# Four graph layers on one core: one-hot products split over the panels of a pass, two whole arms behind a branch, and tiles turned ahead of the last product

## The chip, the cores and the metric

The kernel runs on one core of a Trainium2 chip. The metric is the device time of one execution in microseconds. The core has five engines that work side by side, each with its own queue of instructions: TensorE (PE, matrix products, with its weight loads as PEld), VectorE (DVE), ScalarE (ACT), GpSimd (POOL) and SyncE (SP, which here issues DMA transfers). An engine works through its queue in order; an instruction that waits holds up all behind it.

## What is computed

There are N = 2708 nodes with 128 features each and a dense adjacency matrix `adj` (2708 x 2708, mostly zeros). Four graph layers follow one another, each as `x = layernorm(x + layer(x, adj))`. Cut to what matters here:

```python
# layer 0: z from adj @ x, the 4 nearest neighbours by distance, added to adj
# layer 1: attention; the quotient needs adj @ exp(...) for every pair of nodes
XW = X @ W;  s_col = XW @ a[:f];  s_row = XW @ a[f:]
den = exp(leaky_relu(s_row[:, None] + s_col[None, :], 0.01))
num = A @ den
att = where(num != 0, den / where(num != 0, num, 1), 0)
x = layernorm(x + A @ (att @ XW))
# layer 2
d = 1 / sqrt(adj.sum(axis=1) + 1e-6)
x = layernorm(x + (d[:, None] * adj * d[None, :] @ x) @ W.T + b)
# layer 3
x = layernorm(x + relu(concat([x, adj @ x]) @ W.T + b))
```

The kernel uses that `exp(leaky_relu(r + c))` is one of two products of a row factor and a column factor, depending on the sign of r + c. Nodes are ranked by c and cut into 44 blocks of 62 ranks (`NB`, `BJ`). For one block only the rows whose sign changes inside it need their own weights; the rest enter through sums that are carried from block to block.

## The kernel before

The matrix is held transposed in HBM and read in panels of 4 x 128 rows by up to 512 columns (`load_panel`, 1 MB) into a ring of strips; six of the 22 row tiles stay resident (`res`). The columns are cut into six chunks (`C`), four panels each. The stages follow one another:

1. The first pass with the degrees, the products z, the distances and the four nearest of each node (to about 297 us), and a second pass over the panels for layer 0, during which nodes are ranked (to 484 us).
2. **The third pass** (484 to 569 us). For each chunk `part_sum` (L1056) multiplies every panel by `lc`, 32 columns wide, and `end_sums` (L1065 to L1068) copies the sums to `tot`, folds them with the matrix `sel` and stores them as rows of `carry`. Beside it the lists of the blocks are made. The order on TensorE, VectorE and ScalarE is the written one (`tc.manual_schedule`). `into_places(out, at, values)` compares places with a ramp on VectorE (L906) to get one-hot matrices `hot_in`, in four parts over three buffers, and multiplies the values by them on TensorE (L911), 44 matmuls in one go (22 products, two records each). `ranked()` uses it once, behind the first chunk, to get the row numbers `row_j` and the sorted c (`csort`). `find_values()` and `find_places()` then fill `val_b`, the running sums in `counts`, the largest count as `flag`, and the places `pos`. Behind the second chunk `on_all(g_row, csort)` turns csort into a row that all partitions hold (L813, L814); behind the third `listed()` uses `into_places` again and writes `slot_i`, `slot_e`, `slot_f`, and `on_all(gb, rr)` makes another such row. `weights` (L1023 to L1030) fills `lw` behind the third to fifth chunk.
3. **The branch** (L1174, L1175). Every engine reads `flag` into a register. If a block has more than `KC` = 126 rows, a dense arm is run; otherwise the block arm. The dense arm stands first in the program, the block arm in `Else`. With the inputs given the block arm is taken.
4. **The block arm** (574 to 811 us): 2 halves of the columns by 22 pairs of blocks, 44 steps. Each gathers up to 126 rows per block (`load`, L1161, on POOL) and two carry rows (L1167, SP), multiplies them by `lw` (`find_num`, L1227), takes the inverse on ScalarE as Ln and then Exp (`invert`, L1116 and L1117), corrects it on VectorE (`mix_1`, `mix_2`, `mix_3`: L1124, L1128, L1131), and adds the product with `xws` (`add_up`, L1139). Each step has a wide piece (1024 columns) and a narrow one (330). The order on all five engines is the written one. Ahead of the loop stands `nc.scalar.preload_act_table_set("natural_log_exp_and_others")` (L1217), a set of function tables from which both the Ln and the Exp of `invert` run; in the trace it is one `ACT_TABLE_LOAD`.
5. **The turn.** The second half of the sums is copied to `mT` (L1283), 22 tiles are turned on TensorE (L1293) and scaled on VectorE into `mixed` (L1294). Then `dinv` is computed from the degrees with `inv_sqrt` (L1298, L1299; a square root on ScalarE, L232, and a reciprocal on VectorE). These lines stand behind the branch, outside the manual order, so the scheduler places them.
6. Three more passes over the panels (`by_panels`, L190) for layers 1, 2 and 3, each with a normalization per chunk (which takes a square root on ScalarE), to the end at 1149 us.

Of the kernel before, what the change touches and what calls it, by code (L numbers as in the profile page):

```python
# [52 lines left out]
def kernel(  # L53
# [537 lines left out]
    mis_pool = psum.enter_context(tc.tile_pool(name="mis1", bufs=4, space=bass.MemoryType.PSUM))  # L591
# [205 lines left out]
    with tc.tile_pool(name="rank", bufs=1) as rank:  # L797
# [9 lines left out]
        def on_all(row, col):  # L807

            for o in range(0, row.shape[-1], CW):
                e = min(row.shape[-1], o + CW)  # L810
                ps = mis_tile()
                for k in range(o, e, P):
                    nc.tensor.transpose(ps[:, k - o : k - o + P], col[:, k // P : k // P + 1].to_broadcast([P, P]), ident)  # L813
                nc.scalar.activation(row[:, o:e], ps[:, : e - o], AF.Exp, scale=0.99)  # L814
# [82 lines left out]

        parts = [(t, min(t + 6, T)) for t in range(0, T, 6)]

        def into_places(out, at, values):  # L900

            width = values.shape[-1] * values.shape[-2]
            for t0, t1 in parts:
                n = t1 - t0
                hot = hot_in[:, t0 // 6 % 3 * 6 * P : (t0 // 6 % 3 + 1) * 6 * P].rearrange("p (t k) -> p t k", k=P)
                nc.vector.tensor_tensor(  # L906
                    hot[:, :n, :], iota[:, None, :].to_broadcast([P, n, P]),
                    at[:, t0:t1, None].to_broadcast([P, n, P]), op=ALU.is_equal,
                )
                for t in range(t0, t1):  # L910
                    nc.tensor.matmul(  # L911
                        out[:, :width], lhsT=hot[: pw[t], t - t0, :],
                        rhs=values[: pw[t], t, :, :].rearrange("p a b -> p (a b)"),
                        start=(t == 0), stop=(t == T - 1),
                    )
# [10 lines left out]
        def ranked():  # L926

            js = mis_tile()
            into_places(js, b_j, val_q[:, :, :2, :])
            nc.vector.tensor_scalar_add(row_j, js[:, :NQ], float(OOB))  # L930
            nc.vector.tensor_copy(csort, js[:, NQ : 2 * NQ])
            xws = lwx.tile([P, NQ, D], F32, tag="xws", name="xws")
            nc.gpsimd.memset(xws, 0.0)
            nc.scalar.activation(g_col, csort, AF.Exp, scale=0.99)
            nc.scalar.activation(g_inv, csort, AF.Exp, scale=-0.99)
            return xws
# [61 lines left out]
        def listed():  # L998


            sl = mis_tile()
            into_places(sl, pos, val_b)
            lw = lwx.tile([P, NB, BJ + 2], F32, tag="lw", name="lw")
            in_turn = sl[:, : 3 * NB].rearrange("p (v chain m) -> p v m chain", v=3, m=CH)
            for h in range(2):
                nc.vector.tensor_scalar(
                    slot_i[h].rearrange("p (m chain) -> p m chain", m=CH), in_turn[:, 0], 2.0, 2.0 * OOB + h,
                    op0=ALU.mult, op1=ALU.add,
                )

            for n, (v, at) in enumerate(((slot_e, KC), (slot_f, KC + 1))):
                nc.vector.tensor_scalar_add(
                    v.rearrange("p (m chain) -> p m chain", m=CH), in_turn[:, n + 1], ident[:, at : at + 1]
                )
                nc.vector.tensor_copy(lw[:, :, n], v)
            return lw
# [55 lines left out]

        for c in range(C):
            w = cw[c]
            for i0 in range(0, FULL, 4):
# [8 lines left out]
                if (c, i0) == (0, 8):  # L1084
                    find_sel()
                    find_blocks()
            if c % GROUPS == 0:
                for n in range(c, c + GROUPS):
                    part_sum(n, FULL, 0, res[few(n), FULL - S, cols[n]], few(n), last=n == c)
            if c == 0:  # L1090
                count()
                xws = ranked()
                find_values()
                find_places()
            if c == 1:
                g_row = wide.tile([P, NQ * P], F32, tag="wide", name="g_row")
                on_all(g_row, csort)
            if c == 2:
                lw = listed()
                gb = big.tile([P, N], F32, tag="hT", name="gb")  # L1100
                on_all(gb, rr)
            if 2 <= c < C - 1:
                weights(lw, g_row, range((c - 2) * 16, min((c - 1) * 16, NB), 2))
# [69 lines left out]
    mT = wide.tile([P, N], F32, tag="wide", name="mT")  # L1173
    over = nc.values_load(flag[0:1, 0:1], min_val=0, max_val=N)  # L1174
    with tc.If(over > KC) as full:  # L1175
# [36 lines left out]
    with full.Else():  # L1212
        with (
# [40 lines left out]
            with tc.manual_schedule(engines={e.engine for e in engines}):  # L1254
# [4 lines left out]
                for i, (h, q) in enumerate(steps):  # L1259
# [14 lines left out]
                    errs = {}  # L1274
                    for piece, (c0, w, _) in pieces.items():
                        errs[piece] = mix_1(w, nums[i, piece], invs[i, piece], own)
                        keep(i, piece, errs[piece])
                    for piece in pieces:
                        mix_2(invs[i, piece], errs[piece])
                    for piece, (c0, w, _) in pieces.items():  # L1280
                        mix_3(w, q, invs[i, piece], h * HALF + c0)
                add(len(steps) - 1)
                nc.scalar.copy(mT[:, HALF:], haccs[1][:, :HALF])  # L1283

    acc_pool = ctx.enter_context(tc.tile_pool(name="acc2", bufs=3, space=bass.MemoryType.PSUM))
    mis_pool = ctx.enter_context(tc.tile_pool(name="mis2", bufs=5, space=bass.MemoryType.PSUM))

    hT = big.tile([P, N], F32, tag="hT", name="hT")
    mixed = big.tile([P, T, D], F32, tag="y", name="mixed")
    for t in range(T):  # L1290
        p = pw[t]
        pt = mis_tile()
        nc.tensor.transpose(pt[:p, :D], mT[:, t * P : t * P + p], ident)  # L1293
        nc.vector.tensor_scalar_mul(mixed[:p, t, :], pt[:p, :D], f_out[:p, t : t + 1])  # L1294
    spread(mixed[:, FULL, :])


    nc.vector.tensor_scalar_add(dinv, deg, DEG_EPS)  # L1298
    inv_sqrt(dinv, dinv)  # L1299
    y3 = wide.tile([P, T, D], F32, tag="wide", name="y3")  # L1300

    def end_layer1(c, ts):
        for t in ts:
            p = pw[t]
            pt = mis_tile()
            nc.tensor.transpose(pt[:p, :D], hT[:, t * P : t * P + p], ident)
            nc.vector.tensor_add(xs[:p, t, :], xs[:p, t, :], pt[:p, :D])
        normalize(ts, xs)
        for t in ts:
            nc.scalar.mul(y3[: pw[t], t, :], xs[: pw[t], t, :], dinv[: pw[t], t : t + 1])  # L1310
            if t == FULL:
                spread(y3[:, t, :])
            nc.gpsimd.tensor_add(xs[: pw[t], t, :], xs[: pw[t], t, :], bl_sb[: pw[t]])

    by_panels(rows_of(mixed), into_hT(end_layer1))


    own3 = big.tile([P, T, D], F32, tag="y", name="own3")

    def end_layer2(c, ts):  # L1320
        for t in ts:
            p = pw[t]
            po = linear(t, wl_sb)
            nc.vector.scalar_tensor_tensor(
                xs[:p, t, :], po[:p, :D], dinv[:p, t : t + 1], xs[:p, t, :], op0=ALU.mult, op1=ALU.add
            )
        normalize(ts, xs)
        if ts[-1] == FULL:
            spread(xs[:, FULL, :])

    by_panels(rows_of(y3), into_hT(end_layer2))

    for t in range(T):
        p = pw[t]
        pt = mis_tile()
        nc.tensor.transpose(pt[:, :p], xs[:p, t, :], ident[:p, :p])
        xT = small.tile([P, P], F32, tag="z", name="xT")
        nc.scalar.copy(xT[:, :p], pt[:, :p])
        po = mis_tile()
        nc.tensor.matmul(po[:p, :D], lhsT=xT[:, :p], rhs=wx_sb, start=True, stop=True)  # L1340
        nc.vector.tensor_add(own3[:p, t, :], po[:p, :D], bc_sb[:p])

    last = wide.tile([P, T, D], F32, tag="wide", name="last")

    def end_layer3(c, ts):
        for t in ts:
            p = pw[t]
            po = linear(t, wh_sb)
            nc.vector.tensor_add(own3[:p, t, :], po[:p, :D], own3[:p, t, :])
            nc.vector.scalar_tensor_tensor(  # L1350
                last[:p, t, :], own3[:p, t, :], 0.0, xs[:p, t, :], op0=ALU.max, op1=ALU.add
            )
        normalize(ts, last)
        t0, t1 = ts[0], min(ts[-1] + 1, FULL)
        nc.sync.dma_start(out[t0 * P : t1 * P, :].rearrange("(t p) d -> p t d", p=P), last[:, t0:t1, :])
        if t1 <= ts[-1]:
            nc.sync.dma_start(out[FULL * P :, :], last[:LAST, FULL, :])

    by_panels(rows_of(xs), into_hT(end_layer3))


# [32 lines left out]
```

## Time and profile before

| | us |
|---|---|
| median of 14 runs (1141.54 to 1151.47) | 1147.2 |
| the profiled execution | 1150.52 |
| its span, first to last instruction | 1148.8 |
| third pass | 484 to 568.7 |
| block arm, first to last product | 574.3 to 810.1 |
| three last passes | 817.5 to 1141 |
| busy: TensorE / VectorE / ScalarE / GpSimd | 1020.4 / 652.7 / 346.0 / 278.0 |

The profile gives, for each engine, when each instruction ran, for how long, and which instruction or transfer ended the idle time ahead of it. Busy shares over the whole span are averages over stages with different limits, so the windows by stage are of more use. TensorE's clock is granted by a throttle: 1.0 is full speed, and in some stretches of the third pass it was 0.5. `ACT_TABLE_LOAD` is an instruction of ScalarE that brings in a set of function tables (`LoadActFuncSet` in the program).

### The profile page before, as it was taken

How to read it: one execution, taken by the hardware profiler on the slowest of the kernel's cores; microseconds unless marked ns; L12 is line 12 of the kernel's file. 1: busy time of each engine (PE TensorE's matmuls, PEld its weight loads, DVE VectorE, ACT ScalarE, POOL GpSimd, SP SyncE). 2: the span in 40 equal slices, each digit the busy share in tenths (PEclk: the TensorE clock that was granted, in tenths of full speed). 3: DMA queues.
4: the chain of work that ended last, by engine and by line, in shares of the span. 5: the costliest groups of instructions: out<-in, count | busy, mean ns of one | idle time of the engine just before them, and what ended most of it. 6: DMA issues, size and time to landing. Idle time of an engine off the chain costs nothing.

```text
span 1148.8 us, 11369 instructions
## 1 busy us (share of the span) xinstructions
PE 1020.4 (89%) x3651; PEld 489.9 (43%) x3651; DVE 652.7 (57%) x1388; ACT 346.0 (30%) x632; POOL 278.0 (24%) x268
## 2 busy tenths in 40 slices
PE   1899999999945987597589999999899999999997
PEld 0455544444412545344133333333444644465445
DVE  6885459999412555965069989999321221223122
ACT  0000245555001333513266767666010100011000
POOL 4000000001473762000358875663010100000000
PEclk9899999999976988769789999999999999998999
DMA  9986420000644644467635444543657667573854
GB/s 349 364 296 207 141 71 1 1 0 28 219 135 136 208 133 137 146 208 251 199 97 166 145 136 136 160 127 115 218 184 237 191 228 248 154 226 111 270 168 127
DMA packets 109986, 191.67 MB, mean 167 GB/s; under 512 B 13928, under 2 KB 46978, under 8 KB 109918
## 3 DMA queue, kind: packets, MB, share of 16 engines
q1 hardware_dynamic: 91582, 151.86, 40.3%
q0 software_dynamic: 18336, 39.01, 11.6%
q8 instruction: 30, 0.49, 0.2%
q14 instruction: 38, 0.31, 0.1%
HBM read 215.76 MB, written 4.16 MB: 191 GB/s over the span
## 4 chain that ended last, share of the span: by engine, by line
PE 65%; DVE 10%; DMA 8%; another core or an unknown queue 7%; issue 4%; POOL 3%; ACT 3%; SPq 0%; POOLq 0%; DVEq 0%; ACTq 0%
PE acc L190 30%; PE acc L579 8%; PE acc L397 6%; PE num L1227 6%; PE hacc L1139 5%; POOL rows L1161 2%; DVE both L452 2%; PE acc L569 2%; DMA part<-in_adjT 2%; DMA res<-in_adjT 2%; DMA rows<-carry 2%; PE mis L911 1%; DMA xws<-xw_rows,row_j 1%; PE acc L1056 1%
## 5 line engine op out<-in xcount | busy, mean ns | idle before, releaser
L190 PE MATMUL acc<-part,y 128*128 128x512 f32 (+2 forms) x384 | 159.6, 561 | 2.3 <-DMA part<-in_adjT 1.8
L1161 POOL DMA_INDIRECT rows<-in_adjT,slot_i x88 | 126.8, 1441 | 121.2 <-PE num L1227 57.1
L1227 PE MATMUL num<-rows,lw 128*64 128x512 f32 (+1 forms) x528 | 121.0, 564 | 13.3 <-DMA xws<-xw_rows,row_j 7.2
L1139 PE MATMUL hacc<-inv,xws 128*128 128x512 f32 (+1 forms) x264 | 112.1, 560 | 2.4 <-DVE inv L1131 2.0
L579 PE MATMUL acc<-zT,z 128*128 128x512 f32 (+4 forms) x264 | 106.9, 551 | 0.0
L1124 DVE TENSOR_TENSOR err<-inv,num 128x1024 f32<-128x1024 f32 x88 | 74.8, 856 | 50.3 <-ACT inv L1117 47.4
L608 POOL DMA_INDIRECT got<-y_rows,where x88 | 90.1, 1024 | 52.5 <-issue 23.2
L1116 ACT ACTIVATE inv<-num,plain 128x1024 f32<-128x1024 f32 x88 | 80.5, 915 | 70.3 <-PE num L1227 54.1
L190 PEld LDWEIGHTS acc<-part,y 128*128 128x128 f32 x384 | 72.9, 198 | 67.4 <-issue 56.2
L580 ACT COPY key<-acc 128x512 f32<-128x512 f32 (+3 forms) x132 | 70.2, 534 | 58.1 <-issue 29.8
L397 PE MATMUL acc<-part,y 128*128 128x512 f32 (+2 forms) x192 | 82.4, 582 | 3.7 <-DVE y L237 2.2
L1139 PEld LDWEIGHTS hacc<-inv,xws 128*128 128x128 f32 x264 | 46.8, 190 | 80.6 <-issue 50.0
L190 PE MATMUL acc<-part,xs 128*128 128x512 f32 (+2 forms) x192 | 78.8, 553 | 0.2 <-DMA part<-in_adjT 0.2
L1131 DVE SCALAR_TENSOR_TENSOR inv<-gb,g_inv,inv 128x1024 f32<-128x1024 f32 x88 | 77.1, 917 | 0.0
L224 ACT COPY hT<-acc 128x512 f32<-128x512 f32 (+2 forms) x18 | 9.6, 534 | 220.2 <-PE acc L190 220.2
L190 PE MATMUL acc<-part,mixed 128*128 128x512 f32 (+2 forms) x192 | 75.3, 546 | 0.1
L1227 PEld LDWEIGHTS num<-rows,lw 128*64 128x64 f32 x528 | 39.9, 138 | 75.6 <-issue 52.2
L1128 DVE SCALAR_TENSOR_TENSOR inv<-err,inv 128x1024 f32<-128x1024 f32 x88 | 71.8, 856 | 0.0
L579 PEld LDWEIGHTS acc<-zT,z 128*128 128x128 f32 (+1 forms) x264 | 47.0, 186 | 53.8 <-issue 48.4
L541 POOL TENSOR_TENSOR y<-xs,d2inv 128x2176 f32<-128x2176 f32 (+1 forms) x2 | 4.6, 2322 | 265.1 <-ACT d2inv L539 265.1
L1117 ACT ACTIVATE inv<-inv 128x1024 f32<-128x1024 f32 x88 | 67.6, 768 | 2.8
L581 DVE MAX8 near<-key 128x8 f32<-128x2708 f32 (+1 forms) x22 | 65.4, 2971 | 3.4 <-ACT key L580 3.4
(271 smaller groups left out, 1226.7 us busy)
## 6 DMA issues: line engine op xcount, KB each, us to landing
part<-in_adjT SPq DMA_DIRECT2D x102, 1024.0 KB
part<-in_adjT SPq DMA_DIRECT2D x24, 768.0 KB
part<-in_adjT SPq DMA_DIRECT2D x24, 552.0 KB
res<-in_adjT SPq DMA_DIRECT2D x4, 1280.0 KB
got<-y_rows,where POOLq DMA_INDIRECT x88
rows<-in_adjT,slot_i POOLq DMA_INDIRECT x88
rows<-carry SPq DMA_DIRECT2D x88, 10.6 KB
xw_rows<-xwe POOLq DMA_DIRECT2D x1, 1344.0 KB
```

The costliest lines, as they stand in the source:

```text
L190: nc.tensor.matmul(accs[c][: lhsT.shape[-1], :w], lhsT=lhsT, rhs=src, start=start, stop=stop)
L397: nc.tensor.matmul(accs[c][:, : cw[c]], lhsT=y[:, i, :], rhs=src[:, : cw[c]], start=first, stop=last)
L579: nc.tensor.matmul(pks[c][:p, : cw[c]], lhsT=z2[:, :p], rhs=zT[:, cs], start=False, stop=True)
L580: nc.scalar.copy(key[:p, cs], pks[c][:p, : cw[c]])
L608: nc.gpsimd.indirect_dma_start(out=got[:p, :], out_offset=None, in_=y2_rows[:, :], in_offset=bass.IndirectOffsetOnAxis(ap=where[:p, t, k : ...
L1116: nc.scalar.activation(inv, num[:, :w], AF.Ln, scale=plain[:, 0:1], bias=plain[:, 1:2])
L1124: nc.vector.tensor_mul(err, inv, num[:, :w])
L1128: nc.vector.scalar_tensor_tensor(inv, err, 2.0, inv, op0=ALU.subtract, op1=ALU.mult)
L1131: nc.vector.scalar_tensor_tensor(inv, gb[:, col : col + w], g_inv[:, q : q + 1], inv, op0=ALU.max, op1=ALU.mult)
L1139: nc.tensor.matmul(haccs[:, o:e], lhsT=xws[:, q, :], rhs=inv[:, o:e], start=(q == 0), stop=(q == NQ - 1))
L1161: nc.gpsimd.indirect_dma_start(out=rows[i][:KC, n, :], out_offset=None, in_=adj_half[:, :], in_offset=bass.IndirectOffsetOnAxis(ap=slot_i[ ...
L1227: nc.tensor.matmul(num[n * (BJ + 2) : (n + 1) * (BJ + 2), o:e], lhsT=lw[:, 2 * q + n, :], rhs=rows[i][:, n, c0 + o : c0 + e], start=True, ...
```

## The change

Three edits.

- In the third pass `into_places` is split into `ones_at` (the comparisons) and `into_places(..., n)` (the products of one of four parts). A new function `between(c, i0)` is called behind each group of four row tiles and holds all side work: one part behind each panel, `on_all` in pieces of eight or fewer tiles, `find_values` moved ahead of `count`. The results `js` and `sl` get a PSUM pool of their own with one buffer; `mis1` has three buffers instead of four, the second pass included.
- The branch is turned round (`over <= KC`), so the block arm stands first, and all that follows the branch is written out in both arms: `two_layers` holds the turn, dinv, and the layers 1 to 3. Tiles that were allocated anew behind the branch become views of older ones (`hT = gb`, `mixed` of `carry`, `y3` and `last` of `m_rows`, which also holds `mT`).
- In the block arm the first ten tiles (`EARLY`) are turned and scaled, on ScalarE, ahead of the last product; the last step works piece by piece and does not keep carry rows; the copy of the second half is split in three between ScalarE and VectorE.

```diff
-    mis_pool = psum.enter_context(tc.tile_pool(name="mis1", bufs=4, space=bass.MemoryType.PSUM))
+    mis_pool = psum.enter_context(tc.tile_pool(name="mis1", bufs=3, space=bass.MemoryType.PSUM))
+    js_pool = psum.enter_context(tc.tile_pool(name="places", bufs=1, space=bass.MemoryType.PSUM))
...
+        def ones_at(at, n):
+            t0, t1 = parts[n]
+            w = t1 - t0
+            hot = hot_in[:, n % 3 * 6 * P : (n % 3 * 6 + w) * P].rearrange("p (t k) -> p t k", k=P)
+            nc.vector.tensor_tensor(
+                hot, iota[:, None, :].to_broadcast([P, w, P]), at[:, t0:t1, None].to_broadcast([P, w, P]),
+                op=ALU.is_equal,
+            )
+            return hot
+
+        def into_places(out, hot, values, n):
             width = values.shape[-1] * values.shape[-2]
...
+            t0, t1 = parts[n]
+            for t in range(t0, t1):
+                nc.tensor.matmul(
+                    out[:, :width], lhsT=hot[: pw[t], t - t0, :],
+                    rhs=values[: pw[t], t, :, :].rearrange("p a b -> p (a b)"), start=(t == 0), stop=(t == T - 1),
                 )
...
+        def between(c, i0):
+
+            if (c, i0) == (0, 8):
+                find_sel()
+                find_blocks()
+                work["hot"] = [ones_at(b_j, n) for n in range(3)]
+                find_values()
+            if (c, i0) == (0, 20):
+                count()
+                work["js"] = js_pool.tile([P, CW], F32, tag="places", name="js")
+                into_places(work["js"], work["hot"][0], val_q[:, :, :2, :], 0)
+                work["hot"].append(ones_at(b_j, 3))
+                find_places()
+            if c == 1 and i0 < 12:
+                n = i0 // 4 + 1
+                into_places(work["js"], work["hot"][n], val_q[:, :, :2, :], n)
+            if (c, i0) == (1, 8):
+                work["hot"] = [ones_at(pos, n) for n in range(3)]
+                work["xws"] = ranked(work["js"])
+                work["sl"] = js_pool.tile([P, CW], F32, tag="places", name="sl")
+            if (c, i0) == (1, 20):
+                into_places(work["sl"], work["hot"][0], val_b, 0)
+                work["hot"].append(ones_at(pos, 3))
+                work["g_row"] = wide.tile([P, NQ * P], F32, tag="wide", name="g_row")
+                on_all(work["g_row"], csort, 0, 4)
+            if c == 2 and i0 < 16:
+                if i0 < 12:
+                    into_places(work["sl"], work["hot"][i0 // 4 + 1], val_b, i0 // 4 + 1)
+                n0 = (4, 12, 20, NQ)[i0 // 4]
+                on_all(work["g_row"], csort, n0, n0 + 8)
+            if (c, i0) == (2, 8):
+                work["lw"] = listed(work["sl"])
+            if (c, i0) == (3, 4):
+                work["gb"] = big.tile([P, N], F32, tag="hT", name="gb")
+                on_all(work["gb"], rr, 0, 12)
+            if (c, i0) == (3, 8):
+                on_all(work["gb"], rr, 12, T)
+            if (c, i0) in ((2, 20), (3, 20), (4, 20)):
+                weights(work["lw"], work["g_row"], range((c - 2) * 16, min((c - 1) * 16, NB), 2))
...
+                for t0 in range(0, EARLY, WIDE // P):
+                    ts = range(t0, min(t0 + WIDE // P, EARLY))
+                    pt = ops.tile([P, WIDE], F32, tag=f"num{WIDE}", name="pt", bufs=2)
+                    for t in ts:
+                        nc.tensor.transpose(pt[:, (t - t0) * P : (t - t0 + 1) * P], mT[:, t * P : (t + 1) * P], ident)
+                    for t in ts:
+                        nc.scalar.mul(mixed[:, t, :], pt[:, (t - t0) * P : (t - t0 + 1) * P], f_out[:, t : t + 1])
                 add(len(steps) - 1)
-                nc.scalar.copy(mT[:, HALF:], haccs[1][:, :HALF])
...
+                for o in range(0, HALF, CW):
+                    e = min(HALF, o + CW)
+                    evacuate(o // CW + 1, mT[:, HALF + o : HALF + e], haccs[1][:, o:e])
+
+    def two_layers(arm, first):
...
+        hT = gb
+        for t in range(first, T):
             p = pw[t]
             pt = mis_tile()
...
+        nc.vector.tensor_scalar_add(dinv, deg, DEG_EPS)
+        inv_sqrt(dinv, dinv)
+        y3 = m_rows
...
-    with tc.If(over > KC) as full:
...
+    with tc.If(over <= KC) as fits:
+        with ExitStack() as arm:
+            block_layer()
+            two_layers(arm, EARLY)
+    with fits.Else():
+        with ExitStack() as arm:
+            dense_layer()
+            two_layers(arm, 0)
```

## The prediction

> **What bounds the kernel now.** I read in this order: the windows by stage, the chain of waits, ScalarE's groups and waits in the stage of the blocks, and ScalarE's order of time where tables are loaded. Stages first, since the change touches three: the third pass (484 to 568.7 us), the block arm (574 to 810) and the turn into the next product (810 to 817.5). The columns are the stretch, its length, then busy time of TensorE, weight loads, VectorE, ScalarE and GpSimd, the granted clock, DMA share and GB/s.
>
> ```profile
> span 1148.8 us, 11369 instructions
> 600.00:700.00 100.00, 98.65 (x346) 37.35 (x345) 93.36 (x117) 70.60 (x97) 76.89 (x55) 1.00 0.49 144
> 700.00:808.00 108.00, 105.65 (x374) 40.03 (x373) 103.32 (x129) 70.48 (x84) 54.15 (x37) 1.00 0.46 141
> 484.00:568.70 84.70, 68.02 (x414) 30.70 (x414) 39.14 (x106) 21.56 (x54) 11.97 (x10) 0.80 0.69 223
> ```
>
> In the block arm TensorE and VectorE are both full and one step takes 4.9 us (44 steps). ScalarE is busy 70 of 100 us, so it can take about 1.4 us more per step before it is the bound. Its instructions there, by shape (count | busy, mean ns | idle before), and what it waits for (total us, times, longest):
>
> ```profile
> L1116 ACT ACTIVATE inv<-num,plain 128x1024 f32<-128x1024 f32 x40 | 48.2, 1205 | 32.6 <-PE num L1227 27.3 <-DVE err L1124 4.5 <-issue 0.6
> L1117 ACT ACTIVATE inv<-inv 128x1024 f32<-128x1024 f32 x40 | 42.3, 1057 | 1.3
> L1116 ACT ACTIVATE inv<-num,plain 128x330 f32<-128x330 f32 x40 | 25.1, 627 | 28.4 <-PE num L1227 17.5 <-DVE inv L1131 10.3 <-issue 0.6
> L1117 ACT ACTIVATE inv<-inv 128x330 f32<-128x330 f32 x40 | 19.1, 479 | 1.3
> L1271 ACT ACTIVATE xws<-xws,g_col 128x128 f32<-128x128 f32 x19 | 7.3, 386 | 0.0
> ACT inv L1116 <- PE num L1227: 44.8, 57, 2.2
> ```
>
> Now ScalarE in order of time (start, length): where dinv's square root runs, what a table load costs in the stream, and the arm's entry and end.
>
> ```profile
> 157.36 0.23 ACT L232 ACTIVATE dinv<-dinv 128x22 f32<-128x22 f32 x1
> 159.63 1.28 ACT L557 ACT_TABLE_LOAD   x1
> ...
> 479.05 0.24 ACT L691 COPY xwe<-mis 20x129 f32<-20x129 f32 x1
> 479.31 1.28 ACT L804 ACT_TABLE_LOAD   x1
> 480.60 0.22 ACT L804 ACTIVATE e_r<-rr 128x22 f32<-128x22 f32 x1
> ...
> 568.33 0.38 ACT L1068 COPY carry<-mis 88x276 f32<-88x276 f32 x1 [1.91 <-PE mis L1067]
> 574.36 1.28 ACT L1217 ACT_TABLE_LOAD   x1 [5.65 <-issue]
> 578.20 1.20 ACT L1116 ACTIVATE inv<-num,plain 128x1024 f32<-128x1024 f32 x1 [2.56 <-PE num L1227]
> ...
> 803.69 0.48 ACT L1117 ACTIVATE inv<-inv 128x330 f32<-128x330 f32 x1
> ```
>
> The reader should see two things. The 22-column square root, written behind the branch, runs at 157 us, while the square-root table is still active. And inside the arm one load (L1217) serves all 176 logarithms and exponentials: no other load stands between 578 and 804 us.
>
> **The decisive part: where the square root goes.** The changed kernel writes the next layers inside each arm, so dinv cannot be computed ahead of the branch any more. ScalarE's order in the block arm of the changed kernel as built (no profile; L1248 is the preload, L1143 and L1144 are the Ln and Exp of `invert`, which are L1116 and L1117 before):
>
> ```
> L1248 LoadActFuncSet
> L232 LoadActFuncSet
> L232 Activation dinv<-dinv 128x22
> L1143 LoadActFuncSet
> L1143 Activation inv<-num,plain 128x1024
> L1144 LoadActFuncSet
> L1144 Activation inv<-inv 128x1024
> ```
>
> The square root lands between the preload and the loop and evicts the shared table; after it every Ln and every Exp of the loop has a load of its own, 176 in all. The same listing for the kernel before has 7 loads, and the 6 outside the untaken arm are exactly those in its trace, so the listing counts.
>
> Cost of a load: 479.31 to 480.60 is 1.29, and it starts 0.02 after the previous end; 1.31 us each. ScalarE's work from the first of these loads to the last Exp: 176 x 1.31 = 230.6; activations 44 x (1.205 + 1.057 + 0.627 + 0.479) = 148.2; the xws scalings 22 x 0.386 = 8.5, each overlapping its predecessor by about 0.1 (-2.2); one copy of mT 1.3. Sum 386.4, or 8.6 to 8.9 us per step. Before, the same stretch ran from 578.20 to 804.17, 226.0. **+160.4 us.**
>
> Nothing else should be late in that loop. After the narrow Exp, VectorE still has the short product (0.5), the pair of mix_2 (1.55) and the pair of mix_3 (1.75): 3.8 us, while ScalarE spends 4.9 on the next wide pair with its loads. TensorE needs 2.43 + 2.47 per step at full clock. The gathers (POOL) and carry rows (SP) keep their order and get 8.6 us instead of 4.9 per step.
>
> Two rules of the Trainium skill bear on this. "ScalarE: Activation LUTs", What ACT_TABLE_LOAD costs, gives about 2.66 us for each switch, drain included; by it the loads would be 468 us and the kernel near 1531. The row above shows no drain between load and neighbours. "ScalarE activation tables: per-element evaluation and per-set limits", Table sets in the compiler and the runtime, says the back end places loads per block by the greedy longest run; by that one load would serve the loop and the kernel would gain. The listing shows otherwise.
>
> **Third pass.** Of TensorE's order of time, what this part and the turn below rest on:
>
> ```profile
> 497.97 9.74 PE L911 MATMUL mis<-val_q,hot_in 128*128 128x44 f32 x44
> 522.09 0.92 PE L813 MATMUL mis<-ident,csort 128*128 128x128 f32 x6 [3.47 <-ACT g_row L814]
> 531.14 5.41 PE L911 MATMUL mis<-val_b,hot_in 128*128 128x132 f32 x44
> 543.02 1.27 PE L1067 MATMUL mis<-tot,sel 128*88 128x512 f32 x2 [2.90 <-ACT tot L1065]
> ```
>
> The one-hot products (44 in 9.74 us at a granted clock of 0.5, 44 in 5.41 at 1.0) are only moved between panels. VectorE: in_b ends at 496.7; three comparisons 2.7, find_values 4.5, the fourth 0.7 and the running sums and pos 9 bring pos to 513.7 instead of 521.3; with three comparisons and row_j, csort, 516.8. TensorE has its js parts and the second chunk done by about 508.6 and then waits for csort, because sl takes the bank of js: a new wait of 8 us. From there the third chunk, sl and the csort turns take some 13 us; ScalarE's copy tot again stands behind eight weights (2.75, as at 539.75), so the next fold starts near 532.3 instead of 543.0. The rest took 25.7 us and now also holds gb's turns, 2.6: end at 560.6 instead of 568.7, **-8**. Bounds: -16, all of TensorE's waits in this stage, and +2, if the new wait grows and gb's turns run at half clock. The xws clearing on POOL (2.44) moves from 508 to 517, still 30 us ahead of its gathers. The flag, for which SP waited 2.5 us, comes earlier.
>
> **Entry.** From the last carry copy to the first Ln were 9.5 us, 5.65 of them without any wait that the profile shows, in a jump past the dense arm; now the block arm follows the branch directly. But ScalarE first runs two loads and the root, 2.8 us. No row has a branch not taken: between 0 and -6, I take -5, since most of the 5.65 goes and the first product (3.8) becomes the limit. **-5.**
>
> **Turn.** Before, from the last Exp (804.2) to a running product (817.5) were 13.3 us. Now ten of 22 tiles are scaled on ScalarE while VectorE ends: ten x 0.30 = 3.0, three copies one behind the other 1.7, five turns at 0.25 and evictions, 8.3. **-5** (-2 to -8).
>
> **The jump moves to the end** of the arm: SP and VectorE must jump past the dense arm before the kernel ends. 0 to +7.8 (SP's gap at entry, 554.8 to 562.7, is the nearest row); DMA is idle then, I take **+3**. **One PSUM tile fewer** for the second pass: 0 to +4, the waits of TensorE on xwe copies there are 1.3; **+1**.
>
> Sum: 160.4 - 8 - 5 - 5 + 3 + 1 = +146.4. The profiled execution took 1150.5 us, 3.3 above the median 1147.2; it would become 1297, and the median **1293.6**.
>
> **Rivals.**
> - *TensorE becomes the bound at half clock.* It idles 3.7 us of each 8.6 us step; after 1.7 us idle ahead of 496 the clock was 0.5 until 508. At 0.5 its step is 9.8 us: 44 x 9.8 = 431, 45 above ScalarE's sum, 1339. Against it: a TensorE that is always busy got 1.0 in every long stretch.
> - *A drain or refill at each load that the rows of single loads don't show.* Doubling the load, 176 x 1.31 more: 1524. Against it: all six loads measured 1283 ns.
> - *Not slower: the loads cost almost nothing when they come often,* for instance because both tables stay at hand. The place is ScalarE's 1.45 us of waiting per step (60.8 us in 42 steps); below 0.36 us per load all of it hides, and what is left is -8 - 5 - 5 + 3 + 1: 1133. Against it: the same 1283 ns for every load, whichever table it fetched.
>
> **How the numbers follow.** Loads at the row's price 0.90, TensorE at half clock 0.04, doubled loads 0.03, hidden loads 0.03. The time is that of the first. Its range: lowest bounds together 160.4 - 16 - 6 - 8 = +130, 1277; highest 160.4 + 2 - 2 + 7.8 + 4 = +172, 1319, of which the far end needs every bound at once; I give 1277 to 1316. The other three hold 1 in 10 and lie outside. A measurement of this kernel tells apart about 0.2%, 2.3 us: faster 0.03 (hidden loads), same 0.00, slower 0.97.
>
> **What would show it.** Right: some 183 table loads of 1283 ns; ScalarE busy near 570 us instead of 346 and over 95% in the arm; steps of 8.6 to 8.9 us; VectorE and TensorE waiting for L1144. The third pass ending near 561, a fold waiting for tot, and TensorE waiting for csort ahead of sl. Wrong: steps near 4.9 us (loads hidden), near 9.8 with a clock of 0.5 (TensorE), or 13 and more (drain).

## The result and the profile after

The changed kernel took 1300.4 us in the median (1293.6 to 1302.3, 10 runs); the kernel before took 1147.5 beside it (47 runs). The ratio is 1.132, 95% interval 1.129 to 1.135. The change is slower by 153 us, and the profiled span grew by 152.5, from 1148.8 to 1301.3 us.

From the page and from the groups of the changed kernel (count | busy us, mean ns | idle before):

```profile
span 1301.3 us, 11554 instructions
PE 1053.5 (81%) x3651; PEld 497.5 (38%) x3651; DVE 654.0 (50%) x1379; ACT 576.3 (44%) x820; POOL 265.3 (20%) x268
...
L1143 ACT ACT_TABLE_LOAD x88 | 112.9, 1283 | 2.6 <-issue 1.0
L1144 ACT ACT_TABLE_LOAD x88 | 112.9, 1283 | 1.6
```

ScalarE has 188 more instructions, and 177 of them are table loads: one per logarithm, one per exponential, and the square root's own. 2 x 112.9 = 225.8 us of loads are nearly all of its additional 230 us of busy time. ScalarE in order of time, from the last copy of the third pass into one step of the loop:

```profile
569.30 0.38 ACT L1068 COPY carry<-mis 88x276 f32<-88x276 f32 x1 [1.31 <-PE mis L1067]
569.92 1.28 ACT L1248 ACT_TABLE_LOAD   x1 [0.23 <-issue]
571.21 1.28 ACT L232 ACT_TABLE_LOAD   x1
572.50 0.22 ACT L232 ACTIVATE dinv<-dinv 128x22 f32<-128x22 f32 x1
573.76 1.28 ACT L1143 ACT_TABLE_LOAD   x1 [1.04 <-issue]
...
702.95 0.39 ACT L1302 ACTIVATE xws<-xws,g_col 128x128 f32<-128x128 f32 x1
703.35 1.28 ACT L1143 ACT_TABLE_LOAD   x1
704.65 0.63 ACT L1143 ACTIVATE inv<-num,plain 128x330 f32<-128x330 f32 x1
705.29 1.28 ACT L1144 ACT_TABLE_LOAD   x1
706.58 0.48 ACT L1144 ACTIVATE inv<-inv 128x330 f32<-128x330 f32 x1
707.08 1.28 ACT L1143 ACT_TABLE_LOAD   x1
708.38 1.21 ACT L1143 ACTIVATE inv<-num,plain 128x1024 f32<-128x1024 f32 x1
709.60 1.28 ACT L1144 ACT_TABLE_LOAD   x1
710.90 1.06 ACT L1144 ACTIVATE inv<-inv 128x1024 f32<-128x1024 f32 x1
711.86 0.38 ACT L1302 ACTIVATE xws<-xws,g_col 128x128 f32<-128x128 f32 x1
```

The set that holds both functions is loaded at 569.92 and pushed out 1.3 us later by the square root's. From the first load of the loop on, at 573.76, ScalarE has no gap: a step is 8.9 us (702.95 to 711.86), and the end of one instruction and the start of the next are at most 0.02 us apart, loads included. What the others wait for (total us, times, longest), and the stretch of the loop (busy TensorE, weight loads, VectorE, ScalarE, GpSimd, granted clock, DMA share, GB/s):

```profile
DVE err L1151 <- ACT inv L1144: 168.7, 86, 5.6
PE num L1258 <- DVE err L1151: 80.4, 38, 6.6
...
574.00:960.00 386.00, 255.19 (x778) 90.66 (x776) 215.41 (x261) 380.80 (x375) 132.00 (x101) 0.88 0.30 88
```

ScalarE is busy 98.7% of the loop; VectorE waits for it, and TensorE for VectorE. Stage by stage, from the two traces:

| stretch | before | after | difference |
|---|---|---|---|
| start to the first product of the third pass | 486.1 | 490.1 | +4.0 |
| third pass, to the last copy into carry | 82.6 | 79.6 | -3.0 |
| entry, to the first Ln or its load | 9.5 | 4.1 | -5.4 |
| loop, to the last Exp | 226.0 | 386.7 | +160.7 |
| last Exp to the last VectorE instruction | 341.5 | 335.6 | -6.0 |
| to the end of the span | 3.1 | 5.3 | +2.2 |

### The profile page after: what moved, and what is told of

Same layout as the page of the kernel before. It is cut to its first block, busy times and chain, and to the rows that moved or that the text cites. A ratio compares the mean times of both kernels' runs of the same rounds, so it can differ in the third digit from the quotient of the medians.

```text
span 1301.3 us, 11554 instructions
## 1 busy us (share of the span) xinstructions
PE 1053.5 (81%) x3651; PEld 497.5 (38%) x3651; DVE 654.0 (50%) x1379; ACT 576.3 (44%) x820; POOL 265.3 (20%) x268
## 4 chain that ended last, share of the span: by engine, by line
PE 51%; ACT 20%; DVE 10%; issue 9%; another core or an unknown queue 7%; DMA 3%; SPq 0%; POOL 0%; DVEq 0%; ACTq 0%; POOLq 0%
PE acc L190 27%; PE acc L579 7%; ACT L1143 7%; PE acc L397 5%; ACT inv L1144 5%; ACT inv L1143 5%; DVE both L452 3%; PE acc L569 2%; PE acc L1056 2%; DMA part<-in_adjT 2%; DMA res<-in_adjT 1%; DVE where L582 1%; PE mis L263 1%; DVE inv L1155 1%
## 5 line engine op out<-in xcount | busy, mean ns | idle before, releaser
L1258 PE MATMUL num<-rows,lw 128*64 128x512 f32 (+1 forms) x528 | 131.4, 640 | 81.1 <-DVE err L1151 80.4
L1188 POOL DMA_INDIRECT rows<-in_adjT,slot_i x88 | 119.1, 1353 | 261.3 <-PE num L1258 214.2
L1166 PE MATMUL hacc<-inv,xws 128*128 128x512 f32 (+1 forms) x264 | 131.1, 640 | 50.2 <-ACT xws L1302 42.9
L1143 ACT ACT_TABLE_LOAD x88 | 112.9, 1283 | 2.6 <-issue 1.0
L1144 ACT ACT_TABLE_LOAD x88 | 112.9, 1283 | 1.6
L1166 PEld LDWEIGHTS hacc<-inv,xws 128*128 128x128 f32 x264 | 53.2, 216 | 144.7 <-ACT xws L1302 63.5
L224 ACT COPY gb<-acc 128x512 f32<-128x512 f32 (+2 forms) x18 | 9.6, 534 | 219.4 <-PE acc L190 219.4
L397 PE MATMUL acc<-part,y 128*128 128x512 f32 (+2 forms) x192 | 83.6, 590 | 5.4 <-DMA part<-in_adjT 3.2
L190 PE MATMUL acc<-part,y 128*128 128x512 f32 (+2 forms) x192 | 84.6, 577 | 1.9 <-DMA part<-in_adjT 1.4
L190 PE MATMUL acc<-part,carry 128*128 128x512 f32 (+2 forms) x192 | 74.8, 543 | 0.4 <-DMA part<-in_adjT 0.4
L190 PE MATMUL acc<-part,m_rows 128*128 128x512 f32 (+2 forms) x192 | 74.6, 542 | 0.3 <-DMA part<-in_adjT 0.3
```

Of the source, the lines that this page charges most:

```text
L190: nc.tensor.matmul(accs[c][: lhsT.shape[-1], :w], lhsT=lhsT, rhs=src, start=start, stop=stop)
L397: nc.tensor.matmul(accs[c][:, : cw[c]], lhsT=y[:, i, :], rhs=src[:, : cw[c]], start=first, stop=last)
L1143: nc.scalar.activation(inv, num[:, :w], AF.Ln, scale=plain[:, 0:1], bias=plain[:, 1:2])
L1144: nc.scalar.activation(inv, inv, AF.Exp, scale=-1.0)
L1166: nc.tensor.matmul(haccs[:, o:e], lhsT=xws[:, q, :], rhs=inv[:, o:e], start=(q == 0), stop=(q == NQ - 1))
L1188: nc.gpsimd.indirect_dma_start(out=rows[i][:KC, n, :], out_offset=None, in_=adj_half[:, :], in_offset=bass.IndirectOffsetOnAxis(ap=slot_i[ ...
```

## The experiments

Each kernel ran beside the kernel before, on the same chip. That took 1102 to 1106 us beside the first ten kernels and 1143 beside the last two (root_ahead_again, no_early_tiles), where the prediction had 1147; so ratios and differences are compared, and absolute times that were expected on the basis of 1147 are to be read as differences. Below, *the first runs* are those of the result. *Theory A* is that the square root between preload and loop makes 176 loads, and that they are the whole loss. Its rivals: B, the turned branch and the long arms slow the loop; C, TensorE's clock; D, the entry waits for gathered rows whatever else is saved; E, the early tiles replace other waits or don't count; F, a drain at each load.

All traces in one table, in us: the third pass from first product to last copy into carry; entry from there to the first Ln; loop from first Ln to last Exp; last, from the last Exp to the last VectorE instruction.

| kernel | ratio (95%) | third pass | entry | loop | last | end |
|---|---|---|---|---|---|---|
| before_here | | 78.1 | 9.1 | 227.3 | 340.8 | 3.1 |
| after_here | 1.135 (1.129-1.140) | 72.4 | 6.1 | 385.5 | 335.6 | 5.5 |
| root_alone | 1.154 (1.145-1.162) | 78.5 | 10.7 | 385.4 | 339.7 | 3.1 |
| half_the_loads | 1.041 (1.032-1.049) | 69.5 | 4.3 | 274.1 | 334.0 | 5.9 |
| set_loaded_again | 0.989 (0.985-0.993) | 72.9 | 5.0 | 230.4 | 337.0 | 5.6 |
| all_root_ahead | 0.989 (0.986-0.993) | 73.3 | 3.7 | 228.1 | 335.4 | 5.8 |
| root_behind_loop | 0.992 (0.988-0.996) | 68.0 | 3.6 | 226.2 | 335.6 | 5.3 |
| arms_only | 0.997 (0.994-1.000) | 78.5 | 4.5 | 228.2 | 335.6 | 5.9 |
| arms_and_turn | 0.998 (0.996-1.001) | 79.4 | 3.5 | 222.0 | 337.2 | 5.6 |
| third_pass_alone | 0.993 (0.989-0.997) | 72.6 | 11.1 | 225.3 | 340.9 | 3.1 |
| root_ahead_again | 0.993 (0.991-0.996) | 75.4 | 4.0 | 224.4 | 337.2 | 6.3 |
| no_early_tiles | 0.991 (0.987-0.995) | 79.6 | 4.0 | 226.2 | 338.4 | 5.6 |

### The two kernels again

> The kernel before, unchanged, for its stages on this chip. Its profile was taken where the second pass waited some 30 us for copies of hT (TensorE idle from 330 to 352 us), which no experiment's trace shows. Expected: span 1101 us, the third pass from 446 us on and 78.5 us long, entry 10 us, loop 226 to 228 us, turn 11 to 14 us, end 3.1 us.

> The changed kernel, unchanged, for its time and its stages on this chip. Theory A by the stages measured on this chip: 1103 + 159 for the loop (385.4 against 226) - 8.5 for the third pass - 6 for the entry - 5.5 for the turn + 2.3 for the end = 1244 us (ratio 1.128, between 1.122 and 1.136); the third pass at 68 to 73 us with TensorE's last products, and not a late panel, ahead of the last copy to tot. If instead the 10.25 us that the last copy to tot waited belongs to the change, the third pass takes 79 us here too and the time is 1253 us.

Measured: 1108.0 us in one run of the kernel before (1105.7 in the median of the 14 beside it), and 1256.5 for the changed one. The spans differ by 148.3: 1.5 ahead of the third pass, -5.7, -3.0 to the first Ln, +158.2, -5.2, +2.4 and 0.1 of rounding. The third pass gained 5.7 here and 3.0 in the first runs, where the last copy to tot started late; it does not here.

### The square root alone

```diff
         with (dense arm, block arm)
             ...                          # behind the loop, in each arm
+            nc.vector.tensor_scalar_add(dinv, deg, DEG_EPS)
+            inv_sqrt(dinv, dinv)
     (behind the branch)
-    nc.vector.tensor_scalar_add(dinv, deg, DEG_EPS)
-    inv_sqrt(dinv, dinv)
```

> The kernel before with one thing done: the two lines of dinv moved behind the loop inside both arms, outside the written order; nothing else of the change. As built, the root stands at the arm's entry and each Ln and Exp has a table load. Theory A: +160.7 for the loads and 2.8 at entry for two loads and the root, 1147.4 + 163 = 1310, range 1303 to 1317. Rival B (the turned branch or the long arms cost it): 1147 to 1150.

Measured: ratio 1.154, +169 us (interval 160 to 179), 88 + 88 loads, loop 385.4. The branch is not turned and no other part of the change is there, and the loop is the changed kernel's to 0.1 us. B has nothing left to explain. The profiled execution was the fastest of five, and its span is 159 us above that of before_here.

### Half the loads

The order Ln, Exp, Ln, Exp becomes Ln, Ln, Exp, Exp; the square root stays.

```diff
-                    find_inv(i, "narrow")
-                    if i + 1 < len(steps):
-                        find_inv(i + 1, "wide")
+                    both = [(i, "narrow")] + ([(i + 1, "wide")] if i + 1 < len(steps) else [])
+                    for k in both:
+                        invs[k] = own.tile(...)
+                        nc.scalar.activation(invs[k], nums[k]..., AF.Ln, scale=plain[:, 0:1], bias=plain[:, 1:2])
+                    for k in both:
+                        nc.scalar.activation(invs[k], invs[k], AF.Exp, scale=-1.0)
```

> The changed kernel with ScalarE's order in the loop changed from Ln, Exp, Ln, Exp to Ln, Ln, Exp, Exp, so that a step has two table loads instead of four, 90 in the arm instead of 178. Theory A with the loads at 1.31 us each and ScalarE the only bound: a step takes 3.37 + 2.62 + 0.3 (first half) us, 271 us instead of 386.7: 1300.4 - 116 = 1185, range 1178 to 1195. Rival C (TensorE at half clock is the bound): it stays above 1280. Rival F (a drain beside each load that overlaps when they are dense): more than 1200.

Measured: ratio 1.041, 90 loads in the loop (86 fewer). ScalarE's groups there:

```profile
L1301 ACT ACT_TABLE_LOAD x44 | 56.5, 1283 | 0.8
L1305 ACT ACT_TABLE_LOAD x44 | 56.5, 1283 | 0.8
L1301 ACT ACTIVATE inv<-num,plain 128x1024 f32<-128x1024 f32 x43 | 51.8, 1204 | 7.0 <-PE num L1258 7.0
```

The loop went from 385.5 to 274.1, so a load is worth 111.4 / 86 = 1.30 us while ScalarE is the bound, 1.283 of it the instruction. Working the prediction's sum with 90 loads gives 117.9 + 148.2 + 7.6 = 273.7; with its first load the loop took 275.4. Neither F (a drain) nor hidden loads fit. C is out too: by it the time stays that of the changed kernel, above 1280 where the kernel before took 1147, and it fell to 1147.4 beside 1102.0. With 90 loads ScalarE is still the bound, but already waits 7.0 us for TensorE's num.

### The square root elsewhere, or its place kept and the set loaded once more

all_root_ahead moves dinv's two lines ahead of the branch. root_behind_loop puts them at the end of the block arm's written order (and of the dense arm). set_loaded_again leaves them alone and moves one other line:

```diff
-            nc.scalar.preload_act_table_set("natural_log_exp_and_others")
             nums, invs, haccs = {}, {}, {}
 ...
                 find_inv(0, "wide")
+                nc.scalar.preload_act_table_set("natural_log_exp_and_others")
                 for i, (h, q) in enumerate(steps):
```

> The changed kernel with one thing undone: dinv is computed ahead of the branch, so its square root runs early and the arm keeps the shared tables. Theory A (the 176 table loads are the whole loss): the block arm falls back to steps of 4.9 us, 226 us from the first Ln to the last Exp instead of 386.7; 1300.4 - 160.7 - 1.5 (two loads and the root at entry) = 1138, range 1134 to 1143, and 6 table loads in the trace. Rival B (the turned branch or the longer arms slow the block arm itself): steps stay well above 4.9 us, 1200 or more. Rival C (TensorE at half clock is the bound of the arm): it too falls, but the clock in the arm before must then have been near 0.5.

> The changed kernel with the root left inside the arms but written behind the loop, at the end of the arm's written order. Theory A (it is the place of the root, not that it stands in the arm): 1 table load at the arm's entry and one behind the loop, which the normalization then needs no more; within 2 us of the kernel with the root ahead, 1138, range 1134 to 1143. If standing inside an arm is what costs: near 1300.

> The changed kernel with one line moved: the table set that holds both functions is loaded behind the first piece of the first step, and not ahead of the loop; the square root stays where the changed kernel has it, between the third pass and the loop. Theory A (the square root's own set pushes the shared set out, and each Ln and each Exp then gets its own load, because the set last loaded does not hold it): only the first piece loads twice, 174 of 176 loads go, the loop takes 226 + 2.6 = 229 us where it took 386.7, and the time is that of the two kernels with the root elsewhere, 1091 to 1097 us (ratio 0.989 to 0.995). Rival B (the length of the arm or the turned branch is what makes the loop slow): the loop stays near 385 us and the time near 1255 us (ratio 1.138). A second rival, that any square root in the arm spoils the choice of sets for all of the loop: the same, near 1255 us.

Measured: 0.989, 0.992 and 0.989 of the kernel before; the loops take 228.1, 226.2 and 230.4 us. ScalarE of set_loaded_again in order of time:

```profile
521.90 1.28 ACT L232 ACT_TABLE_LOAD   x1 [0.23 <-issue]
523.19 0.22 ACT L232 ACTIVATE dinv<-dinv 128x22 f32<-128x22 f32 x1
525.36 1.28 ACT L1143 ACT_TABLE_LOAD   x1 [1.95 <-issue]
526.66 1.20 ACT L1143 ACTIVATE inv<-num,plain 128x1024 f32<-128x1024 f32 x1
527.88 1.28 ACT L1144 ACT_TABLE_LOAD   x1
529.18 1.06 ACT L1144 ACTIVATE inv<-inv 128x1024 f32<-128x1024 f32 x1
530.25 1.28 ACT L1289 ACT_TABLE_LOAD   x1
531.54 0.63 ACT L1143 ACTIVATE inv<-num,plain 128x330 f32<-128x330 f32 x1
532.20 0.48 ACT L1144 ACTIVATE inv<-inv 128x330 f32<-128x330 f32 x1
532.59 1.19 ACT L1143 ACTIVATE inv<-num,plain 128x1024 f32<-128x1024 f32 x1
```

The root runs where the changed kernel has it, the first Ln and Exp load as they do there, and then one load at 530.25 ends it: 1094.8 us instead of 1256.5 beside it on one chip, 161.7 us for one line. The rival that any square root in the arm spoils the loop is out as well, since in root_behind_loop the arm holds it too. Loads in the loop come from what the last set loaded ahead of it holds, and from nothing else that was changed. These three show what the rest of the change is worth: each beats both kernels.

### The arms and the early tiles

arms_only is the kernel before with the branch turned, both arms to the end and the root ahead of the branch; arms_and_turn adds the ten early tiles and the split copy. no_early_tiles is all_root_ahead without the ten tiles:

```diff
-                for t0 in range(0, EARLY, WIDE // P):
-                    ...                      # ten transposes on TensorE, ten scalings on ScalarE
-            two_layers(arm, EARLY)
+            two_layers(arm, 0)
```

> The kernel before with the branch turned round and both arms written to the end, the root ahead of the branch, no change of the third pass and no tiles turned early. Theory A: the entry gains 5 and the jump at the end costs 2.2, so 1147.4 - 3 = 1144, range 1140 to 1148. Rival D (the entry waits for the gathered rows, not for the jump): the entry gains 0 to 1, and with the jump at the end 1149.

> The same with the ten tiles turned ahead of the last product and the copy split, the third pass still as before. Theory A: 5 less than with the arms only, 1139, range 1135 to 1143; from the last Exp to the running product 8 us instead of 13. The kernel with all three edits should then be another 3 to 8 us below. Rival E (the tiles turned early only take the place of other waits): no more than 1 us below the arms only.

> The kernel of all_root_ahead without the ten tiles turned ahead of the last product (all 22 are turned behind it, in the arm). Theory E (the early tiles give the gain at the turn, 5 us): from the last Exp to the end of the last pass 340.5 us where the kernel with early tiles takes 335.5, and 0.994 of the kernel before. Rival E' (the gain at the turn comes from writing the turn in the arm, where the passes' first products stand behind 6 turned tiles instead of 18; this is what the stages of arms_only, 335.6 us without early tiles, and of arms_and_turn, 337.2 us with them, speak for): 335.5 us, and the same ratio as the kernel with early tiles, within 0.002.

> The kernel of all_root_ahead a second time, to stand beside the next one on the same chip. Theory A: 0.989 of the kernel before, between 0.985 and 0.993.

Measured: arms_only is 3.0 us faster (interval -6.2 to +0.1), arms_and_turn 1.8 (-4.7 to +1.2). In the traces the arms shorten the entry by 4.6 us and the last stretch by 5.2, and lengthen the end by 2.8. The kernels before_here and arms_only ran on different chips, but the other two traces with the old branch, root_alone and third_pass_alone, one from each chip, have 10.7 and 11.1 at the entry and 339.7 and 340.9 in the last stretch, so the chip does not make it. These stages add up to -7.0, more than arms_only gained in time; what takes up the rest is not shown. D falls: the entry does not wait for gathered rows. Without early tiles the last stretch is 335.6 and 338.4 us, with them 334.0 to 337.2, and no_early_tiles is no slower than its neighbour (0.991 against 0.993). So the early tiles are worth nothing that these runs can tell; in the traces the gain comes with the arm. TensorE at the turn, before_here and then arms_only:

```profile
769.64 4.20 PE L1293 MATMUL mis<-ident,mT 128*128 128x128 f32 x18 [1.38 <-ACT mT L1283]
773.68 1.02 PE L190 MATMUL acc<-part,mixed 128*128 128x512 f32 x2
```

```profile
763.98 1.10 PE L1300 MATMUL mis<-ident,m_rows 128*128 128x128 f32 x6 [1.38 <-ACT m_rows L1289]
764.92 1.02 PE L190 MATMUL acc<-part,carry 128*128 128x512 f32 x2
765.78 0.49 PE L1300 MATMUL mis<-ident,m_rows 128*128 128x128 f32 x3
```

Before, 18 of the 22 tiles are turned ahead of the first product of layer 1; in the arm it is six, though all 22 are still turned behind the loop. That accounts for 3.1 of the 5.2 us; the scheduler placed them so, and what in the arm made it was not tried.

### The third pass alone

The changed kernel's lines down to the end of the third pass, with the branch, loop and turn of the kernel before.

> The kernel before with the third pass of the changed kernel (the products in parts between the panels, mis1 with three buffers), and the branch, the loop and the turn as they were. Theory T (the third pass is ended by TensorE's own work and its waits, so whatever is taken out of it is gained): the stretch from the first product of the third pass to the last copy into carry was 78.5, 79.4 and 78.5 us in the three kernels with the old order and 73.3, 68.0 and 69.5 us in the three with the new one on this chip; expected 70 us here, the entry unchanged at 9.5 to 10.7 us, and 1094 us against 1103 of the kernel before (ratio 0.992, between 0.987 and 0.996). Rival D (the block arm's first rows come late whatever the third pass does): the entry grows by what the pass loses, and the time stays at 1103 (0.998 to 1.002). Theory A expects 0 table loads in the loop and the loop at 222 to 228 us, since the square root stays behind the branch.

Measured: ratio 0.993, 8.0 us faster (3.2 to 12.7); the pass 72.6 us against 78.1, the entry 11.1 against 9.1. D, by which the entry takes the whole gain back, is excluded. Beside a kernel before of 1102 to 1106 us the pass took 78.1 to 79.4 in the old order (four traces) and 68.0 to 73.3 in the new one (six). What goes with the spread of the six is TensorE's clock. The stretches around 460 us in third_pass_alone and, second, in root_behind_loop (columns as above):

```profile
464.00:468.00 4.00, 4.00 (x18) 3.01 (x20) 3.38 (x18) 0.58 (x1) 0.00 (x0) 0.50 0.79 262
468.00:472.00 4.00, 4.00 (x20) 2.64 (x12) 3.72 (x10) 0.00 (x0) 0.00 (x0) 0.50 0.36 88
472.00:476.00 4.00, 4.00 (x21) 2.14 (x24) 0.88 (x1) 0.00 (x0) 0.00 (x0) 0.50 0.67 212
476.00:480.00 4.00, 4.00 (x17) 0.86 (x18) 2.87 (x5) 0.33 (x2) 2.45 (x1) 0.50 0.82 277
```

```profile
464.00:468.00 4.00, 4.00 (x33) 2.85 (x32) 3.37 (x17) 0.58 (x1) 0.00 (x0) 1.00 0.83 267
468.00:472.00 4.00, 4.00 (x35) 1.79 (x35) 3.76 (x8) 0.00 (x0) 1.62 (x1) 1.00 0.98 347
472.00:476.00 4.00, 1.33 (x9) 0.45 (x5) 3.43 (x6) 0.33 (x2) 0.83 (x1) 1.00 1.04 386
```

The same lines run in both. In all six the granted clock falls to 0.50 between 457 and 460 us. Where it stays there until 481 to 483, for 24 us, TensorE is not idle from 460 to 480 and the pass takes 72.4 to 73.3 us (four traces); where it is back after 7 us, at 464 or 467 (root_behind_loop, half_the_loads), TensorE gets ahead and waits for csort, and the pass takes 68.0 and 69.5. In root_behind_loop:

```profile
471.13 1.88 PE L1056 MATMUL acc<-res,lc 128*32 128x512 f32 x10
475.68 1.59 PE L916 MATMUL sl<-val_b,hot_in 128*128 128x132 f32 x12 [2.67 <-DVE csort L933]
```

## Why the prediction was right

1293.6 us was predicted, 1300.4 measured, inside the range of 1277 to 1316; the sum of the steps was +146.4, measured were +153.0 in the first runs and +150.7 in after_here. That the root's place would cost a load per function was read from the built order and priced by a row, and both held; the smaller terms held less well. In the first runs the third pass gained 5.0 us less than forecast and 4.0 us came ahead of it; the other terms take back some 3.

- **Loop, +160.4.** Measured +160.7; the working (176 loads of 1.31, the activations, 386.4 together) met 386.7. The signs held: 183 loads of 1283 ns, ScalarE busy 576 us, 98.7% of the arm, steps of 8.9 us. Nothing else became late in the loop.
- **The drain.** "ScalarE: Activation LUTs", What ACT_TABLE_LOAD costs (the Trainium skill), gives some 2.66 us for a switch, drain included. Here the groups have 4.2 us of idle ahead of 176 loads and 2.2 ahead of the 176 activations, 0.02 and 0.01 us each, and half_the_loads gives 1.30 us for a load; the measurement decides.
- **Where loads are placed.** "ScalarE activation tables: per-element evaluation and per-set limits", Table sets in the compiler and the runtime (the Trainium skill), has the back end choose the greedy longest run. Ln and Exp alternate for 176 instructions, and after the root they got 176 loads, though set_loaded_again shows that one serves 174 of them. In this build the run is served only if the shared set was asked for and still stands.
- **Third pass, -8.** Measured -3.0, in after_here -5.7, and -8.0 in time for this part alone; within the bounds of -16 to +2. The step that failed in the first runs is the timetable: the js parts and the second chunk were to be done by 508.6, followed by a wait of 8 us for csort. The pass began 4.0 us later here, which makes that 512.6. TensorE instead ran at a granted 0.57 from 500 to 524 and reached sl at 523.54. Csort came close to its forecast, at 521.4 against 516.8 + 4.0, so the predicted wait was filled with slow products. Where the clock came back early the wait is there, with 2.67 us. The fold's wait for tot in midpass was 0.36 us. At the end another wait took its place (last section).
- **Entry, -5.** Measured -5.4 and, in after_here, -4.3 to the first load. arms_only shows it comes from the turned branch.
- **Turn, -5.** Right in size (-6.0 and -5.2 with the passes), wrong in cause: the prediction put it down to ten tiles scaled while VectorE ends, but the arms give 5.2 without them. That this term came out is luck.
- **End, +3** measured +2.2 and +2.4. **One PSUM tile fewer, +1**: from the end of the second pass's first copy of hT to the third pass were 128.4 us against 128.9 in the first runs. In the traces beside 1102 to 1106 us TensorE's waits for xwe copies in the second pass are 1.24 us with three buffers and 0.76 with four, in the first runs 1.24 and 1.28; so it is half a microsecond at most that this shows.
- **Rivals.** TensorE at half clock did appear, 0.88 on average over the loop, but its products still ended ahead of ScalarE's. The reason given against it, that a TensorE that is always busy got 1.0 in every long stretch, was wrong already in the trace before: from 496 to 508 us TensorE was busy for 11.8 of 12 us at a granted 0.50. The rival fell because the clock averaged 0.88, with TensorE busy for 255 of 386 us, and not for that reason. Doubled and hidden loads are out by half_the_loads.

The 4.0 us ahead of the third pass are there by the last product of the distances (286.7 and 291.2 us), in code that the change does not touch, and were 1.5 in after_here.

## What to carry to other kernels

A table set that is loaded by hand serves a loop only as long as nothing with another set lands behind it: after moving any function across a branch or into a scheduled region, count the loads in the built order, and write the load into a fixed order behind everything that the scheduler may pull forward. A loss this size can hide a gain: freed of the loads, the same change is 0.7 to 1.1% faster than the kernel before. And a gain that comes out in the right size can still be another part's; only leaving the part out shows it.

## What the runs showed that was not expected

**A clock that stays at half under load.** In four kernels TensorE's records show it busy without a gap from 460 to 480 us at a granted 0.50. "TensorE: Matmul & The Clock Gate", Part 1: The HAM clock gate (the Trainium skill), has full speed return after a busy window of some 3.4 us, with a phase that varies from run to run. By that rule another phase moves the return by one window at most. Here the same lines came back after 7 us in two kernels and after 24 in four, and 20 us of a busy TensorE at 0.50 do not fit; the measurement decides. Some of the matmuls there are short (44 columns) or use 32 columns of weights (lc), and busy is not full use; what the gate counts, no run here shows.

**A ScalarE that wakes late, in some runs.** In the second pass of the kernel before:

```profile
356.63 0.58 ACT L739 COPY hT<-acc 128x512 f32<-128x512 f32 x1 [59.41 <-remote]
...
357.27 1.01 PE L653 MATMUL mis<-w,hT 128*128 128x128 f32 x3 [28.90 <-ACT hT L739]
```

TensorE's last product ahead of this ended at 328.4; ScalarE, idle for 59 us, began the copy 28 us later. All four traces from where the kernel before took 1143 to 1147 us show it (59.2 to 59.4 us), none of the ten others, whichever kernel ran, and it is most of the 38 us by which the third pass begins later in the trace of before than in before_here. The last copy to tot has it too. In the changed kernel:

```profile
560.18 1.09 PE L1056 MATMUL acc<-res,lc 128*32 128x276 f32 x10
568.04 1.22 PE L1067 MATMUL mis<-tot,sel 128*88 128x276 f32 x2 [6.77 <-ACT tot L1065]
```

In those four traces tot starts 2.4 us (before) and 6.2 to 6.9 us (new order) after its last product, in the others 0.1. That is why the third pass gained so little there: without these late starts the first runs would have had some 7 us instead of 3.0, an estimate from 82.6 - 2.4 and 79.6 - 6.3. The profile cannot name what ended either wait, and the cause stays open.
